# Finishing the blocks of one half inside the next half's loop (layers 1 and 2 of a four-layer graph network)

## The chip, the cores and the metric

The kernel runs on one core of a Trainium2 chip. The engines of the core work side by side, each from its own queue: PE (TensorE) multiplies matrices into banks of the accumulation memory, DVE (VectorE) and ACT (ScalarE) do elementwise work, POOL (GpSimd) does some small operations and issues some transfers, SP (SyncE) issues the transfers of the big rows. Sixteen DMA engines carry all transfers. The metric is the device time of one execution in microseconds (us): 891.3 us as the median of three runs (887.4 to 891.43) before the change. The profiled execution took 884.95 us, with a span of 883.1 us in its trace.

## The reference

There are 2708 nodes with 128 features each, and a dense 0/1 matrix `adj` of 2708 x 2708 in float32. Four layers follow each other, each of the form x = x + layer(relu(layernorm(x))). The change touches layers 1 and 2:

```
# layer 1
adj_hat = adj + eye
d = (rowsum(adj_hat) + 1e-8) ** -0.5
out = relu(((d[:,None] * adj_hat * d[None,:]) @ h) @ weight)      # x += out

# layer 2
deg = rowsum(adj), 0 replaced by 1
agg = adj.T @ h / deg[:,None]
g = agg @ W_n.T + b_n + h @ W_c.T + b_c
out = relu(gamma * (g - mean(g)) / sqrt(var(g) + 1e-5) + beta)    # mean, var over nodes; x += out
```

Layer 0 is an attention layer, whose row sums of `adj` give the degrees. Layer 3 is another attention layer, in which sorting by a score takes the place of a dense product of exponentials; it takes more than half of the time, and the change leaves it alone.

## The kernel before, in words

The 2708 rows of the matrix are cut into T = 22 row tiles of 128 (the last has 20), and the 2708 columns into six blocks of 512 (the last has 148). One block is one accumulation bank.

A product of layers 1 and 2 runs in `product_by_halves`. The columns are taken in two halves: half 0 is blocks 0 to 2 (1536 columns), half 1 is blocks 3 to 5 (1172 columns). In each half a loop goes over the 22 row tiles. For each tile the rows of `adj` (or of its transpose) are loaded (768 KB or 586 KB), converted to a rounded float type [...], and multiplied into the three banks of the half. The node features h stand as the stationary operand, cut into a high and a low part (`h_hi`, `h_lo`, written by `cut_in_two`), so each block takes two matmuls per tile (line 225).

The loads land in eight buffers in turn: three in `dflat`, one in `row_b` (layer 1) or `hn` (layer 2), and four of the pool `raws`. The transfers are issued by SP in program order (line 77). The conversion on line 525 takes turns between ACT and DVE (the first five of a layer are all on ACT) and writes to the pool `ring` of six buffers; a load buffer is free as soon as it is converted. The conversions keep their program order. Everything else is placed on the engines' queues by a scheduler that may move it.

The first 18 tiles of a half are multiplied tile by tile; the last four (NLAST) are loaded together and multiplied block by block. After its last four tiles each block is finished:

- In layer 1 `finish1` evacuates the bank to `yT` (lines 216 and 218, DVE for odd and ACT for even blocks), multiplies by the weight (line 571, PE), scales and applies relu (line 573, ACT), adds to x (line 575, DVE), and does the layer norm of the next layer. That is: statistics on DVE (lines 185 and 186), variance plus epsilon (173, DVE), the power -0.5 (174, POOL), the shift (190, DVE), and scaled relu on ACT (192). The result `h2` (in `hs`) is the features of layer 2, which `cut_in_two` (lines 501 and 502, DVE) then splits.
- In layer 2 `finish2` multiplies the bank by 1/degree of each column (line 602, DVE, from `row_a`), multiplies by the two weights (604 and 605, PE), adds the bias (606, ACT), and takes statistics (607, DVE). It needs `hT`, the transposed features, which `turn` makes from `h2` by PE transposes (199) and a copy (598).

At the start of layer 1 `finish0` does the last step of layer 0 block by block: transposes, division by the denominators (557), and the layer norm, with a factor `dis` multiplied in on DVE (189). Block 0 is done before the loop, the others at every fourth tile.

`row_a`, which only `finish2` needs, holds 1/degree along the columns, the same in every partition. It is made by two transfers that POOL issues at the head of the layer: line 484 writes `rdeg` (128 partitions x 22 numbers, node t*128+p at [p, t]) to the memory outside in the order of the nodes, 2816 pieces of 4 bytes; line 485 reads it back into all partitions (1354 KB). The second waits for the first to land.

Of the kernel before, what the change touches and what calls it, by code (L numbers as in the profile page):

```python
# [8 lines left out]
F32 = mybir.dt.float32  # L9
# [10 lines left out]
def kernel(  # L20
# [19 lines left out]
    nc = tc.nc  # L40
    P = 128
    N, D = x.shape
    assert D == P
    T = -(-N // P)
# [11 lines left out]
    TILES = [range(c // P, min(c // P + 4, T)) for c, _ in E0]  # L56
# [3 lines left out]
    NLAST = 4  # L60
# [19 lines left out]
    def cols(t):  # L80
        return slice(t * P, (t + 1) * P)
# [7 lines left out]
    small = ctx.enter_context(tc.tile_pool(name="small", bufs=2))  # L89
# [4 lines left out]
    def bank():  # L94
        return ps.tile([P, 512], F32, tag="bank", name="bank")
# [14 lines left out]
    ident = const.tile([P, P], F32, name="ident")  # L110
# [7 lines left out]
    def load(name, shape, src, queue):  # L118
        t = const.tile(shape, F32, name=name)
        queue.dma_start(t, src)  # L120
        return t
# [36 lines left out]
    hn = big.tile([P, T, D], F32, name="hn")  # L158
# [3 lines left out]
    row_a = big.tile([P, NPAD], F32, name="row_a")  # L162
# [18 lines left out]
    def layernorm(b, dst, factor=None):  # L181

        ts = slice(TILES[b][0], TILES[b][-1] + 1)
        for t in TILES[b]:
            nc.vector.bn_stats(st[:, t, :], xs[:, t, :])
            nc.vector.bn_aggr(mv[:, t, :], st[:, t, :])
        inv_sqrt(rstd[:, ts], mv[:, ts, 1], 1e-5)
        if factor is not None:
            nc.vector.tensor_mul(rstd[:, ts], rstd[:, ts], factor[:, ts])
        nc.vector.scalar_tensor_tensor(shift[:, ts], mv[:, ts, 0], -1.0, rstd[:, ts], ALU.mult, ALU.mult)  # L190
        for t in TILES[b]:
            nc.scalar.activation(
                dst[:, t, :], xs[:, t, :], AF.Relu, bias=shift[:, t : t + 1], scale=rstd[:, t : t + 1]
            )
# [25 lines left out]
    def aggregate(stationary, moving, accs, start, stop, blocks=range(NB), at=0):  # L220
        parts = stationary if isinstance(stationary, list) else [stationary]
        for b in blocks:
            lo, hi = E0[b]
            for i, w in enumerate(parts):
                nc.tensor.matmul(  # L225
                    accs[b][:, : hi - lo],
                    w,
                    moving[:, lo - at : hi - at],
                    start=start and i == 0,
                    stop=stop and i == len(parts) - 1,  # L230
                )
# [14 lines left out]
                aggregate(stationary(t), a, accs, False, t == order[-1], [b])  # L246
            finish(b, accs[b])

    def product_by_halves(order, stationary, load, finish, extra, after):

        for h, (h0, _) in enumerate(COLS):
            blocks = range(3 * h, 3 * h + 3)
            accs = {b: acc_bank(b) for b in blocks}
            for i, t in enumerate(order[:-NLAST]):
                a = load(t, h)
                aggregate(stationary(t), a, accs, i == 0, False, blocks, h0)
                if t // 4 in blocks:
                    extra(t, accs)
                after(i, h)
            last = [(t, load(t, h)) for t in order[-NLAST:]]  # L260
            for b in blocks:
                for t, a in last:
                    if t in TILES[b]:
                        extra(t, accs)
                    aggregate(stationary(t), a, accs, False, t == order[-1], [b], h0)
                finish(b, accs[b])

    with ExitStack() as stack:
        stream = stack.enter_context(tc.tile_pool(name="stream", bufs=NSTREAM))
# [22 lines left out]
        for b in range(NB):  # L292
            layernorm(b, hn)
            p = bank()
            turned(p, hn, TILES[b])
            nc.vector.tensor_copy(hT[:, spans(b)], p[:, : len(TILES[b]) * P])
            p = acc_bank(b % 2)
# [29 lines left out]
        accs = [acc_bank(b) for b in range(NB)]  # L327
# [13 lines left out]
        for t in range(T):  # L341
            a = first_rows[t] if t < 3 else load_rows(adj, t)
# [48 lines left out]
        p = bank()  # L391
# [20 lines left out]
        rdeg = const.tile([P, T], F32, name="rdeg")  # L412
# [17 lines left out]
    rdeg_d = dram.tile([NPAD], F32, name="rdeg_d")  # L430
# [49 lines left out]
    def rest(exact, stack3):  # L480

        nc.gpsimd.dma_start(rdeg_d.rearrange("(t p) -> p t", p=P), rdeg)
        nc.gpsimd.dma_start(row_a[:, :N], rdeg_d[:N].partition_broadcast(P))
        s12 = stack3.enter_context(ExitStack())
        ring = s12.enter_context(tc.tile_pool(name="ring", bufs=6))
        raws = s12.enter_context(tc.tile_pool(name="raws", bufs=4))
        h2 = hs[:, :, :P]
# [7 lines left out]
        def cut_in_two(h, b):  # L497

            if exact:
                ts = slice(TILES[b][0], TILES[b][-1] + 1)  # L500
                nc.vector.tensor_copy(h_hi[:, ts, :], h[:, ts, :])
                nc.vector.tensor_sub(h_lo[:, ts, :], h[:, ts, :], h_hi[:, ts, :])  # L502

        def halves_of(h):
            return lambda t: [h_hi[:, t, :], h_lo[:, t, :]] if exact else [h[:, t, :]]
# [26 lines left out]
        next_row = loader(adj_t, [*three, row_b[:, :CUT]], 3)  # L532
# [32 lines left out]
        def finish1(b, acc):  # L565
            evacuate(b, yT, acc)
            n = len(TILES[b])
            p = bank()
            o = stage.tile([P, 4, P], F32, tag="o", name="o", bufs=2)
            for q, t in enumerate(TILES[b]):  # L570
                nc.tensor.matmul(p[:, cols(q)], yT[:, cols(t)], w1_sb, start=True, stop=True)
            for q, t in enumerate(TILES[b]):
                nc.scalar.activation(o[:, q, :], p[:, cols(q)], AF.Relu, scale=dis[:, t : t + 1])
            ts = slice(TILES[b][0], TILES[b][-1] + 1)
            nc.vector.tensor_add(xs[:, ts, :], xs[:, ts, :], o[:, :n, :])
            layernorm(b, h2)

            for o in {3: (3,), 5: (4, 5)}.get(b, ()):
                cut_in_two(h2, o)

        def after1(i, h):

            if h == 1 and i in (5, 9, 13):
                cut_in_two(h2, i // 4 - 1)

        product_by_halves(range(T), halves_of(hn), load_plus_one, finish1, plus_one, after1)


        bias = small.tile([P, 1], F32, tag="bias", name="bias")
# [1 line left out]
        st2 = small.tile([P, NB, 6], F32, tag="st2", name="st2", bufs=1)  # L591
        tot = small.tile([P, 8], F32, tag="tot", name="tot", bufs=1)
        def turn(i, h):
            if i in (2, 4, 6):
                b = 3 * h + i // 2 - 1
                p = bank()
                turned(p, h2, TILES[b])
                nc.vector.tensor_copy(hT[:, spans(b)], p[:, : len(TILES[b]) * P])
# [8 lines left out]
            nc.vector.bn_stats(st2[:, b, :], row_b[:, lo:hi])  # L607

        next_row = loader(adj, [*three, hn.rearrange("p t d -> p (t d)")[:, :CUT]])
        product_by_halves(range(T), halves_of(h2), next_row, finish2, lambda t, accs: None, turn)  # L610
        nc.vector.bn_aggr(tot[:, 0:2], st2)
        inv_sqrt(tot[:, 4:5], tot[:, 1:2], 1e-5)
        nc.vector.tensor_mul(tot[:, 5:6], vecs[:, 2:3], tot[:, 4:5])
# [42 lines left out]
        with tc.tile_pool(name="tab", bufs=1) as tab, tc.tile_pool(name="tabs", bufs=2) as tabs:  # L656
# [17 lines left out]
            for b in range(NB):  # L674
# [4 lines left out]
                p = acc_bank(b % 2)  # L679
# [10 lines left out]
                p = acc_bank(2 + b % 2)  # L690
# [10 lines left out]
                for c in range(new.start, new.stop, 3):  # L701
# [8 lines left out]
                    p = acc_bank(4)  # L710
# [5 lines left out]
            for c in range(0, T, 3):  # L716
# [9 lines left out]
                for q in range(m):  # L726
                    t = c + q
# [15 lines left out]
                    o = (t % 4) * P  # L743
# [5 lines left out]
            p = bank()  # L749
# [33 lines left out]
            accs = [acc_bank(b) for b in range(3)]  # L783
# [72 lines left out]
            p = acc_bank(3)  # L856
# [4 lines left out]
            p = acc_bank(4)  # L861
# [10 lines left out]
            p = acc_bank(3)  # L872
# [32 lines left out]
            def sums_before(name, x):  # L905
# [45 lines left out]
            order = row("order")  # L951
# [20 lines left out]
                tag="w3",  # L972
# [21 lines left out]
            p = acc_bank(4)  # L994
# [121 lines left out]
        accs = [acc_bank(b) for b in range(NB)]  # L1116
# [89 lines left out]
        for b in range(NB):  # L1206
            evacuate(b, y_t, accs[b])
            p = bank()
# [91 lines left out]
```

## Time and profile before

| stretch of the trace (us) | what runs | length |
|---|---|---|
| 0 to 204 | layer 0 | 204 |
| 204 to 227.4 | start of layer 1, up to the first tile's matmul | 23.4 |
| 227.4 to 264.4 | layer 1, half 0 | 37.0 |
| 264.4 to 278.5 | its blocks are finished | 14.1 |
| 278.5 to 311.3 | layer 1, half 1 | 32.8 |
| 311.3 to 324.1 | its blocks are finished | 12.8 |
| 324.1 to 358.6 | layer 2, half 0 | 34.5 |
| 358.6 to 391.4 | its blocks, and layer 2, half 1 | 32.8 |
| 391.4 to 883.1 | end of layer 2, layer 3 | 491.7 |

The page gives, for the whole span, the busy share of each engine: PE 84%, DVE 66%, ACT 61%, POOL 22%. These are means over stages that differ, so the stages have to be read one by one. In a timeline, a line gives the start in us, the length, the engine, the line of the kernel, the operation, output<-input with sizes, and how many instructions are merged; in brackets stands how long the engine idled before, and what ended that idle time. In the windows a line gives, for a stretch A:B, its length and the busy time of each engine with the number of instructions, then the granted clock of PE as a share of full speed, the busy share of the DMA engines, and the GB/s that they moved.

### The profile page before, as it was taken

How to read it: one execution, taken by the hardware profiler on the slowest of the kernel's cores; microseconds unless marked ns; L12 is line 12 of the kernel's file. 1: busy time of each engine (PE TensorE's matmuls, PEld its weight loads, DVE VectorE, ACT ScalarE, POOL GpSimd, SP SyncE). 2: the span in 40 equal slices, each digit the busy share in tenths (PEclk: the TensorE clock that was granted, in tenths of full speed). 3: DMA queues.
4: the chain of work that ended last, by engine and by line, in shares of the span. 5: the costliest groups of instructions: out<-in, count | busy, mean ns of one | idle time of the engine just before them, and what ended most of it. 6: DMA issues, size and time to landing. Idle time of an engine off the chain costs nothing.

```text
span 883.1 us, 8728 instructions
## 1 busy us (share of the span) xinstructions
PE 739.1 (84%) x2980; PEld 428.5 (49%) x2980; DVE 580.9 (66%) x1097; ACT 536.9 (61%) x595; POOL 196.0 (22%) x161
## 2 busy tenths in 40 slices
PE   3599999992695979987759986389999999989996
PEld 2333333341584857665324321255555555545785
DVE  5599888893734442437986987457666666664844
ACT  3899999991846363437780024278878877866100
POOL 3000000011201010002000011456766665630010
PEclk9799999995796979997679998689999999999999
DMA  8053455707996959996501985477777777785994
GB/s 328 2 190 135 180 189 189 296 11 117 336 394 235 366 207 407 374 381 248 192 0 64 389 326 195 171 290 279 280 269 268 266 267 265 273 319 221 417 427 141
DMA packets 39506, 218.61 MB, mean 248 GB/s; under 512 B 5150, under 2 KB 14030, under 8 KB 25390
## 3 DMA queue, kind: packets, MB, share of 16 engines
q1 hardware_dynamic: 27704, 150.19, 45.4%
q0 software_dynamic: 8656, 65.76, 20.4%
q10 hardware_dynamic: 3090, 1.99, 0.7%
q8 instruction: 26, 0.43, 0.2%
q14 instruction: 30, 0.25, 0.1%
HBM read 214.12 MB, written 3.79 MB: 247 GB/s over the span
## 4 chain that ended last, share of the span: by engine, by line
PE 14%; DMA 11%; DVE 9%; POOL 7%; issue 7%; ACT 5%; POOLq 0%; DVEq 0%; ACTq 0%
DMA hs<-in_adj_t_dram 4%; PE acc L797 3%; PE bank L1178 3%; PE acc L1122 2%; DMA row_b<-pre_d,pre_i 2%; DMA yT<-pre_d,pre_i 2%; POOL hs L634 2%; ACT rows L1140 2%; PE acc L225 2%; POOL hT L634 2%; PE bank L1068 1%; DVE bits L731 1%; POOL yT L634 1%; POOL row_b L634 1%; POOL xw L634 1%
## 5 line engine op out<-in xcount | busy, mean ns | idle before, releaser
L1178 PE MATMUL bank<-rows,d_hi 128*128 128x512 f32 (+1 forms) x264 | 107.4, 411 | 38.4 <-DVE d_hi L1147 17.7
L225 PE MATMUL acc<-rows,h_hi 128*128 128x512 f32 (+1 forms) x264 | 102.7, 395 | 17.2 <-ACT rows L525 16.1
L1122 PE MATMUL acc<-e,xw 128*128 128x512 f32 (+1 forms) x264 | 104.3, 545 | 0.0
L1183 ACT ACTIVATE ln<-bank,tiny 128x512 f32<-128x512 f32 x132 | 79.5, 632 | 32.4 <-PE bank L1178 32.2
L1178 PE MATMUL bank<-rows,d_lo 128*128 128x512 f32 (+1 forms) x264 | 99.0, 386 | 0.0
L225 PE MATMUL acc<-rows,h_lo 128*128 128x512 f32 (+1 forms) x264 | 97.8, 385 | 0.2 <-DVE h_lo L502 0.2
L1178 PEld LDWEIGHTS bank<-rows,d_hi 128*128 128x128 f32 x264 | 51.6, 195 | 67.8 <-ACT ln L1183 31.3
L1186 DVE TENSOR_TENSOR e<-e,ln 128x1536 f32<-128x1536 f32 (+2 forms) x66 | 69.7, 1095 | 19.3 <-ACT ln L1183 19.1
L352 DVE SCALAR_TENSOR_TENSOR tau<-tau,e_hi,a 128x1536 f32<-128x1536 f32 (+1 forms) x44 | 70.6, 1623 | 9.7 <-DMA a<-in_adj_dram 5.9
L1122 PEld LDWEIGHTS acc<-e,xw 128*128 128x128 f32 x264 | 48.5, 191 | 52.5 <-issue 52.5
L349 ACT ACTIVATE tau<-row_a,e_neg,e_lo 128x1536 f32<-128x1536 f32 (+1 forms) x44 | 65.7, 1504 | 3.0 <-PE bank L361 2.8
L225 PEld LDWEIGHTS acc<-rows,h_hi 128*128 128x128 f32 x264 | 52.1, 197 | 30.1 <-ACT rows L525 19.3
L361 PE MATMUL bank<-tau,ones_at 128*32 128x512 f32 (+1 forms) x264 | 51.8, 566 | 8.3 <-DVE tau L352 8.3
L225 PEld LDWEIGHTS acc<-rows,h_lo 128*128 128x128 f32 x264 | 52.0, 197 | 10.1 <-DVE h_lo L502 0.7
L225 PE MATMUL acc<-yT,hs 128*128 128x512 f32 x132 | 55.8, 560 | 0.0
L1192 ACT ACTIVATE e<-e 128x2708 f32<-128x2708 f32 x22 | 54.2, 2463 | 2.2 <-DVE e L1186 2.2
L225 PE MATMUL acc<-row_b,hs 128*128 128x512 f32 x132 | 55.3, 557 | 0.0
L1178 PEld LDWEIGHTS bank<-rows,d_lo 128*128 128x128 f32 x264 | 51.9, 197 | 7.0
L225 PE MATMUL acc<-rows,y_hi 128*128 128x512 f32 x132 | 49.2, 380 | 5.0 <-DVE rows L1255 3.1
L525 ACT CAST rows<-dflat 128x1536 fp32r<-128x1536 f32 (+1 forms) x26 | 34.2, 1332 | 24.9 <-DMA dflat<-in_adj_dram 13.9
L225 PE MATMUL acc<-rows,y_lo 128*128 128x512 f32 x132 | 47.7, 377 | 0.0
L1161 DVE TENSOR_SCALAR xw<-xw,c_exp 128x128 f32<-128x128 f32 x22 | 6.6, 298 | 57.8 <-DMA xw<-xw_d,xw_i 57.8
(406 smaller groups left out, 1418.4 us busy)
## 6 DMA issues: line engine op xcount, KB each, us to landing
a<-in_adj_dram SPq DMA_DIRECT2D x21, 1354.0 KB
rows<-in_adj_t_dram SPq DMA_DIRECT2D x17, 1354.0 KB
dflat<-in_adj_t_dram SPq DMA_DIRECT2D x9, 768.0 KB
rows<-in_adj_t_dram SPq DMA_DIRECT2D x9, 768.0 KB
dflat<-in_adj_dram SPq DMA_DIRECT2D x9, 768.0 KB
rows<-in_adj_dram SPq DMA_DIRECT2D x9, 768.0 KB
dflat<-in_adj_t_dram SPq DMA_DIRECT2D x5, 1354.0 KB
hs<-in_adj_t_dram SPq DMA_DIRECT2D x5, 1354.0 KB
```

Of the source, the lines that this page charges most:

```text
L225: nc.tensor.matmul(accs[b][:, : hi - lo], w, moving[:, lo - at : hi - at], start=start and i == 0, stop=stop and i == len(parts) - 1,)
L349: nc.scalar.activation(tau[:, :w], row_a[:, h0:h1], AF.Relu, bias=e_neg[:, t : t + 1], scale=e_lo[:, t : t + 1])
L352: nc.vector.scalar_tensor_tensor(tau[:, :w], tau[:, :w], e_hi[:, t : t + 1], a[:, h0:h1], ALU.add, ALU.mult)
L361: nc.tensor.matmul(den[g : g + 32, : hi - lo], ones_at[:, b // GR, :], tau[:, lo - h0 : hi - h0], start=(t == 0 and b < GR), stop=(t == T ...
L525: m = nc.vector.tensor_copy(r, a) if i % 2 and i > 4 else nc.scalar.copy(r, a)
L634: return nc.gpsimd.indirect_dma_start(out=out, out_offset=None, in_=src, in_offset=bass.IndirectOffsetOnAxis(ap=idx, axis=0),)
L797: nc.tensor.matmul(accs[b][64 * h : 64 * h + 2 * NC, : hi - lo], wts[:r, t, :], a[:r, lo:hi], start=(t == 0), stop=(t == T - 1),)
L1122: m = nc.tensor.matmul(accs[b][:, : hi - lo], xw, e[:, lo:hi], start=(s == 0), stop=(s == NE - 1))
L1178: m = nc.tensor.matmul(num[:, : hi - lo], d, a[:, lo:hi], start=(i == 0), stop=(i == len(products) - 1))
L1183: nc.scalar.activation(ln[:, lo:hi], num[:, : hi - lo], AF.Ln, bias=tiny)
L1186: tc.keep_in_program_order(nc.vector.tensor_sub(e[:, beg:hi], e[:, beg:hi], ln[:, beg:hi]))
L1192: tc.keep_in_program_order(nc.scalar.activation(e, e, AF.Exp))
```

## The change

Two things are changed.

First, the blocks of a half are no longer finished at its end. The half ends with all 22 tiles in order, and the finishing of its three blocks is put in a list `ends`. The next half's loop, of the same layer or of the next one, takes one entry of the list after its tiles 1, 4 and 7. Only the very last half (half 1 of layer 2) still takes its last four tiles block by block and finishes its own blocks. The purpose is that the loads and products of the next half go on while a block is finished. As blocks 3 to 5 of layer 1 are then finished in layer 2's first half, `turn` is moved from tiles 2, 4, 6 to tiles 10, 12, 14, and `cut_in_two` for them goes into `finish1`.

Second, 1/degree leaves in another form. PE transposes `rdeg` to 22 partitions x 128 numbers, DVE copies it out of the bank, and POOL writes it as 22 rows of 512 bytes. In the program this stands after tile 2 of layer 1's first half, and the broadcast into `row_a` after tile 16 of its second half.

```diff
-    def product_by_halves(order, stationary, load, finish, extra, after):
+    def product_by_halves(stationary, load, finish, extra, after, ends, last):
         for h, (h0, _) in enumerate(COLS):
             blocks = range(3 * h, 3 * h + 3)
             accs = {b: acc_bank(b) for b in blocks}
-            for i, t in enumerate(order[:-NLAST]):
+            at_end = NLAST if last and h else 0
+            for t in range(T - at_end):
                 a = load(t, h)
-                aggregate(stationary(t), a, accs, i == 0, False, blocks, h0)
-                if t // 4 in blocks:
+                aggregate(stationary(t), a, accs, t == 0, t == T - 1, blocks, h0)
+                if t // 4 in blocks and t < T - 1:
                     extra(t, accs)
-                after(i, h)
-            last = [(t, load(t, h)) for t in order[-NLAST:]]
-            for b in blocks:
-                for t, a in last:
-                    if t in TILES[b]:
-                        extra(t, accs)
-                    aggregate(stationary(t), a, accs, False, t == order[-1], [b], h0)
-                finish(b, accs[b])
+                if t == T - 2 and (T - 1) // 4 in blocks:
+                    extra(T - 1, accs)
+                if ends and t in (1, 4, 7):
+                    ends.pop(0)()
+                after(t, h)
+            if at_end:
+                rest = [(t, load(t, h)) for t in range(T - at_end, T)]
+                for b in blocks:
+                    for t, a in rest:
+                        aggregate(stationary(t), a, accs, False, t == T - 1, [b], h0)
+                    finish(b, accs[b])
+            else:
+                ends += [lambda b=b, acc=accs[b]: finish(b, acc) for b in blocks]
...
-        nc.gpsimd.dma_start(rdeg_d.rearrange("(t p) -> p t", p=P), rdeg)
-        nc.gpsimd.dma_start(row_a[:, :N], rdeg_d[:N].partition_broadcast(P))
...
             layernorm(b, h2)
-            for o in {3: (3,), 5: (4, 5)}.get(b, ()):
-                cut_in_two(h2, o)
-        def after1(i, h):
-            if h == 1 and i in (5, 9, 13):
-                cut_in_two(h2, i // 4 - 1)
-        product_by_halves(range(T), halves_of(hn), load_plus_one, finish1, plus_one, after1)
+            if b >= 3:
+                cut_in_two(h2, b)
+        def after1(t, h):
+            if (t, h) == (2, 0):
+                p = bank()
+                nc.tensor.transpose(p[:T, :P], rdeg, ident)
+                by_tile = small.tile([T, P], F32, tag="by_tile", name="by_tile", bufs=1)
+                nc.vector.tensor_copy(by_tile, p[:T, :P])
+                nc.gpsimd.dma_start(rdeg_d.rearrange("(t p) -> t p", p=P), by_tile)
+            if (t, h) == (16, 1):
+                nc.gpsimd.dma_start(row_a[:, :N], rdeg_d[:N].partition_broadcast(P))
+            if h == 1 and t in (6, 10, 14):
+                cut_in_two(h2, t // 4 - 1)
+        ends = []
+        product_by_halves(halves_of(hn), load_plus_one, finish1, plus_one, after1, ends, False)
...
         def turn(i, h):
-            if i in (2, 4, 6):
-                b = 3 * h + i // 2 - 1
+            if i in (10, 12, 14):
+                b = 3 * h + i // 2 - 5
...
-        product_by_halves(range(T), halves_of(h2), next_row, finish2, lambda t, accs: None, turn)
+        product_by_halves(halves_of(h2), next_row, finish2, lambda t, accs: None, turn, ends, True)
```

## The prediction

> **What bounds the kernel now.** I first read the slices of the span: around slices 10, 13 and 15 PE and DMA both sink. The windows by stage then give the shares. The six stretches are layer 1's first half, the gap after it, its second half, the gap before layer 2, and layer 2's two halves (columns: length, busy time of PE, weight loads, DVE, ACT, POOL, clock, DMA share, GB/s):
>
> ```profile
> 227.40:264.40 37.00, 35.66 (x159) 29.26 (x159) 19.78 (x60) 24.50 (x31) 4.17 (x4) 0.93 0.97 365
> 264.40:278.50 14.10, 3.15 (x26) 2.77 (x25) 8.49 (x37) 9.98 (x27) 3.02 (x3) 0.69 0.45 169
> 278.50:311.30 32.80, 32.25 (x168) 27.33 (x168) 11.76 (x25) 13.15 (x15) 2.04 (x2) 0.92 0.98 368
> 311.30:324.10 12.80, 6.72 (x20) 3.50 (x20) 8.50 (x30) 7.20 (x18) 1.75 (x3) 0.75 0.36 150
> 324.10:358.60 34.50, 32.63 (x133) 25.94 (x134) 8.87 (x11) 17.09 (x12) 1.38 (x1) 0.95 0.97 372
> 358.60:391.40 32.80, 32.28 (x154) 24.59 (x154) 13.29 (x20) 14.54 (x14) 1.08 (x1) 1.00 0.94 365
> ```
>
> Inside a half PE is full and DMA nearly so. The gaps are chains: PE idles 10.6 us in the first, some 6 us in the second. Ahead of all this lies a dead stretch, in the timeline of 203 to 226 us:
>
> ```profile
> 204.67 1.61 POOL L484 DMA_DIRECT2D rdeg_d<-rdeg  x1 [3.46 <-issue]
> ...
> 207.35 0.16 DVE L173 TENSOR_SCALAR isq<-mv 128x4 f32<-128x4 f32 x1
> ...
> 221.12 0.60 POOL L485 DMA_DIRECT2D row_a<-rdeg_d  x1 [14.84 <-DMA rdeg_d<-rdeg]
> 221.75 2.02 POOL L174 TENSOR_TENSOR rstd<-isq,neg_half 128x4 f32<-128x4 f32 x2
> 222.81 0.16 DVE L189 TENSOR_TENSOR rstd<-rstd,dis 128x4 f32<-128x4 f32 x1 [12.90 <-POOL rstd L174]
> ```
>
> The power for block 0's normalisation (L174) has its input at 207.5 us, but stands on POOL's queue behind the issue of the broadcast (L485), which waits until the 4-byte scatter (L484) has landed. DVE, ACT and PE all wait for that power. The first gap is a chain too:
>
> ```profile
> 264.38 1.98 PE L571 MATMUL bank<-w_sb,yT 128*128 128x128 f32 x16
> 266.76 1.16 PE L571 MATMUL bank<-w_sb,yT 128*128 128x128 f32 x8 [0.40 <-ACT o L573]
> 278.47 0.79 PE L225 MATMUL acc<-rows,h_hi 128*128 128x512 f32 x1 [10.55 <-ACT rows L525]
> ```
>
> The tile PE waits for is a mere conversion (L525) of rows that landed long ago; it stands on ACT behind three blocks' normalisations.
>
> **What the Trainium skill says.** "DMA: Bandwidth & Descriptors", section Specifications: below 512 B a transfer runs under line rate. The trace agrees: the 11 KB of L484 took 15.9 us in 4-byte pieces. The same page, section Latency and other measured facts: about 2 us fixed cost per DMA; here the 64 KB gathers land in 2.6 us at the median. "TensorE: Matmul & The Clock Gate", section "Architectural detail: the array is 16× 32×32, not 1× 128×128": the queues of ACT and DVE are strictly first in, first out, GpSimd's too for each of its processors; both waits above agree. Its section What's actually happening: an idle window of about 3.4 us halves the clock, a busy one restores it. Here the clock was 0.50 by 272 us, 4 us into the gap, and the first tile after it ran at half rate.
>
> **The change, part by part.**
>
> *1. 1/degree.* Removed: the 4-byte scatter. Added: one transpose (4 such took 1.1 us), one copy of 22x128 (under 0.2 us), a transfer of 22 rows. I looked at the order in which the changed kernel's instructions are built: the scheduler does not leave the broadcast at tile 16 but puts it early again. POOL's queue reads: power block 0, rows out, power block 1, broadcast, power block 2. So block 0 no longer waits for any transfer, and the broadcast still falls in the ramp. The rows' landing is not in the trace: bounds are 2.6 us (the gather) and 15.9 us (the old scatter). I take 2.6, since 22 pieces replace 2,816. Then block 2's power is held until about 214.5, and block 2 serves only tile 8, which PE reaches at 213 + 8 x 1.6 = 226.
>
> Start of PE: from the power's start (221.75) to the first tile (227.39) passed 5.64 us. Now the power starts at 207.4, so PE starts at 213.0, 14.4 us earlier. The eight tiles in flight were asked for by 207.8; eight less the three already there are 3.9 MB, 9.4 us at the 418 GB/s of the full windows, so they are in at about 214. I take off 0.6 us, because DVE used the old wait to prepare part of block 1 and 2: 13.8 us. The half itself stays PE's: 22 tiles x 1.36 us, plus 12 x 0.2 for the identity, plus transposes of five blocks at 1.1 is near the 37.0 measured.
>
> *2. End of layer 1's first half* (X = its last matmul, 264.4 before). The text says "a block at tiles 1, 4, 7", but the built order is different. PE: block 0's weight product, tiles 0 and 1, the products of blocks 1 and 2, then tile 2. ACT: outputs and normalisation of block 0, conversions of tiles 2 and 4, outputs of blocks 1 and 2, normalisation of block 1, tile 6, normalisation of block 2, tile 8. So conversions still queue behind normalisations. Walked with the trace's durations (evacuation 0.58, product 1.16, outputs 1.14, add 0.68, statistics 1.3, power 1.0, normalise 1.65, conversion 1.17 on ACT and 0.77 on DVE, tile 1.15):
>  - PE: product to X+1.2, tiles 0 and 1 to X+3.5, products to X+5.9.
>  - Block 0: outputs to X+2.8, add and statistics to 4.8, power 6.1, normalised 8.1, tile 2 converted 9.2. PE idles 3.4 us.
>  - Outputs of block 1 follow at X+11.4; DVE's add, a cut of h2 into high and low that waits for PE's tile 3, statistics and power bring tile 5 to about X+17.4 and, with tiles 2 and 3 at half clock (+1.5), X+18.9. PE idles another 4 us. Block 2 likewise holds tile 8 to X+25.
>  - Then PE is free: tile 11 ends at X+30, and ten tiles at 1.36 end the half at X+43.5.
>
> Before, the same point is at 311.2, X+46.8, with the products of blocks 3 and 4 (2.3 us) already inside. Gain 3.3 us, of which 2.3 return below.
>
> *3. Layer 1 to 2* (Y = that end). PE: tile 0, products of blocks 3 to 5 around tile 1, the twelve transposes of `turn` hoisted to here, then tile 2. ACT gives tile 2's conversion (1.48 us in this half) only after block 3's normalisation: outputs to Y+7.6, power 10.2, normalised 12.2, converted 13.7, the tile at half clock from Y+14.7. Twenty tiles x 1.36, two `wc` products of 1.05 and about 1.4 more for half clock and a wait for tile 5 end the half at about Y+45.3. Before it took 358.6 - 311.2 = 47.4, with less of these products in it. Both halves together: 94.2 us before, 43.5 + 45.3 = 88.8 now: 5.4 us.
>
> *4. Layer 2's end.* `finish2` of blocks 0 to 2 moves among the tiles: 4 products of 1.05 that stood in front of the half, now inside. PE was full there (32.28 of 32.80), so they cost the same in either place. Rows come at 1.4 us a tile against PE's 1.15 plus these, and lead by several tiles: nought. The last four tiles are as before.
>
> Sum: 13.8 + 5.4 = 19.2 us. 891.3 - 19.2 = 872.1. Layer 3 hangs on layer 2's last block and shifts whole.
>
> **The rivals.**
>  - *The ends overlap fully.* PE's idle 10.6 and 6 us, and some 4 us of half clock, vanish too: 14 + 20.6, 857 us. For it: 97% DMA shows loads would follow, and rings are deep. Against it: the built order above, with ACT and DVE first in, first out.
>  - *Only the start gains.* The scattered waits of PE at each boundary equal the old gap, or the clock halves once more in each (2 us): 14 less 0 to 4, 877 to 881 us. For it: the chain of one block is some 8 us and three now run one after another, where the old order ran three nearly together.
>  - *Slower.* The rows land no faster than the old scatter: issued at 211.5, landed at 227.4, tile 8 then at 232 instead of 226, loss 6; and each boundary costs 9 us more than before, because three block chains in series stand before tile 8: 891.3 - 13.8 + 6 + 18 = 901 us. Against it: piece count, and blocks 0 and 1 pass ahead of that wait.
>
> **How the numbers follow.** Forecast (about 866 to 876 us) 0.55, full overlap 0.17, start alone 0.22, slower or no change 0.06. The range 857 to 881 reaches to the middle of the second and the end of the third, and leaves out some 0.17. The landing of the rows (2.6 to 15.9) costs nothing at one end and 6 us at the other, inside it. Faster by over 0.5% (below 886.8) takes all of the first three and a little is kept back: 0.93; same 0.03; slower 0.04.
>
> **What would show it.** In the trace after: no POOL wait above 4 us before the first power, PE's first tile near 213 us; the old 10.55 us idle on a conversion split into two or three of 2 to 5 us, each put down to ACT or DVE `rows`, DVE `shift` waiting for POOL behind them; layer 2's first half ending near 339, its last matmul near 372. It is wrong if PE runs through the boundaries without such waits (then about 857), if tile 8 of the first half waits for POOL, or if single waits grow past 6 us.

## The result, and the profile after

The changed kernel took 863.5 us (median of 4 runs, 861.0 to 865.7), against 890.6 for the kernel before on the same chip: ratio 0.970 (0.966 to 0.974). Run again beside the experiments it took 863.95 against 884.56, ratio 0.976 (0.971 to 0.981). Measured in pairs the gain is thus 27 and 21 us; it is the kernel before whose median moved (884.6 to 890.6 over the chips used here), not the changed one. The traces say where the gain is made (ends of the tile loops, in us from the span's start):

| end of | before | after | gain so far | forecast |
|---|---|---|---|---|
| wait for the first tile (its matmul starts) | 227.4 | 212.6 | 14.8 | 14.4 |
| layer 1, half 0 | 264.5 | 253.6 | 10.9 | 13.8 |
| layer 1, half 1 | 311.2 | 294.8 | 16.4 | 17.1 |
| layer 2, half 0 | 358.6 | 338.5 | 20.1 | 19.2 |
| layer 2, half 1 | 391.4 | 370.6 | 20.8 | 19.2 |
| span | 883.1 | 860.4 | 22.7 | 19.2 |

What follows layer 2's loop is the same code in both and took 491.7 and 489.8 us; over all thirteen traces of this study it took 487.4 to 494.8. So a whole time says less about this change than the stretch up to 391 us does, and below I read both. One run is left out below: of the four of the kernel called *GpSimd free*, one took 891.4 us at a granted clock of 0.82, where the others show 0.94.

The windows of the kernel after, one for each half with the boundary ahead of it inside (same columns as in the prediction):

```profile
212.60:253.60 41.00, 37.75 (x164) 29.87 (x165) 22.58 (x75) 25.10 (x32) 6.12 (x7) 0.92 1.00 389
253.60:294.80 41.20, 34.03 (x177) 29.01 (x177) 17.98 (x52) 22.02 (x38) 4.11 (x4) 0.92 0.85 304
294.80:338.50 43.70, 38.83 (x170) 30.47 (x169) 19.13 (x51) 25.32 (x34) 4.40 (x4) 0.92 0.98 380
338.50:370.60 32.10, 31.81 (x154) 24.69 (x154) 13.68 (x20) 13.25 (x13) 1.08 (x1) 1.00 0.94 376
```

Two things are to be seen. In the first line DMA is at 1.00 and PE no longer full (37.75 of 41.00; before it was 35.66 of 37.00): this half now runs at what its transfers give. In the second DMA falls to 0.85 and PE to 34 of 41: the boundary still costs something there.

The start of layer 1 after, in the timeline:

```profile
207.99 1.01 POOL L174 TENSOR_TENSOR rstd<-isq,neg_half 128x4 f32<-128x4 f32 x1 [6.46 <-DVE isq L173]
...
210.99 0.86 POOL L591 DMA_DIRECT2D rdeg_d<-by_tile  x1 [2.00 <-DVE mv L186]
...
212.62 1.22 PE L225 MATMUL acc<-rows,h_hi 128*128 128x512 f32 x2 [0.77 <-ACT rows L529]
```

The first block's power starts at 208.0 instead of 221.75, ahead of any transfer of GpSimd's, and PE starts at 212.6. The boundary between the halves of layer 1, PE's waits in its timeline:

```profile
262.24 0.50 PE L225 MATMUL acc<-rows,h_hi 128*128 128x512 f32 x1 [3.45 <-ACT rows L529]
270.52 0.80 PE L225 MATMUL acc<-rows,h_hi 128*128 128x512 f32 x1 [3.02 <-DVE rows L529]
276.29 0.51 PE L225 MATMUL acc<-rows,h_hi 128*128 128x512 f32 x1 [0.69 <-ACT rows L529]
```

In place of one wait of 10.55 us there are three, 7.2 us together. ACT's timeline beside it shows why:

```profile
254.76 1.16 ACT L577 ACTIVATE o<-bank,dis 128x128 f32<-128x128 f32 x4
259.49 1.65 ACT L192 ACTIVATE hs<-xs,shift,rstd 128x128 f32<-128x128 f32 x4 [3.57 <-DVE shift L190]
261.04 2.22 ACT L529 CAST rows<-dflat 128x1172 fp32r<-128x1172 f32 x2
263.17 2.15 ACT L577 ACTIVATE o<-bank,dis 128x128 f32<-128x128 f32 x8
269.82 1.65 ACT L192 ACTIVATE hs<-xs,shift,rstd 128x128 f32<-128x128 f32 x4 [4.50 <-DVE shift L190]
```

ACT stands idle for 3.57 and 4.50 us ahead of a normalisation (L192) whose shift is not there yet, and the conversion PE wants (L529, at 261.0) is queued behind it. In this time the buffers are not given back: from 263.6 to 270.5 us the load queue issues nothing, and DMA moves 0 to 19 GB/s from 268.5 to 271.

### The profile page after: what moved, and what is told of

The parts are those of the page before. It is cut to its first block, busy times and chain, and to the rows that moved or that the text cites. A ratio compares the mean times of both kernels' runs of the same rounds, so it can differ in the third digit from the quotient of the medians.

```text
span 860.4 us, 8730 instructions
## 1 busy us (share of the span) xinstructions
PE 737.2 (86%) x2981; PEld 427.3 (50%) x2981; DVE 580.9 (68%) x1098; ACT 536.0 (62%) x595; POOL 191.8 (22%) x161
## 4 chain that ended last, share of the span: by engine, by line
PE 17%; DMA 11%; DVE 10%; issue 6%; POOL 5%; ACT 5%; POOLq 0%; DVEq 0%; ACTq 0%
PE bank L1191 5%; DMA hs<-in_adj_t_dram 4%; PE acc L1135 4%; DMA row_b<-pre_d,pre_i 4%; PE acc L810 3%; ACT rows L1153 2%; PE acc L225 2%; PE bank L1081 2%; POOL hs L647 1%; POOL hT L647 1%; DVE bits L744 1%; POOL xw L647 1%; POOL row_b L647 1%; ACT e L1205 1%; DMA hs<-in_adj_t_dram,row_i 1%
## 5 line engine op out<-in xcount | busy, mean ns | idle before, releaser
L1191 PE MATMUL bank<-rows,d_hi 128*128 128x512 f32 (+1 forms) x264 | 105.6, 404 | 37.9 <-DVE d_hi L1160 17.4
L225 PE MATMUL acc<-rows,h_hi 128*128 128x512 f32 (+1 forms) x264 | 105.8, 405 | 11.6 <-ACT rows L529 6.3
L1199 DVE TENSOR_TENSOR e<-e,ln 128x1536 f32<-128x1536 f32 (+2 forms) x66 | 69.7, 1096 | 14.8 <-ACT ln L1196 14.4
L529 ACT CAST rows<-dflat 128x1536 fp32r<-128x1536 f32 (+1 forms) x26 | 34.2, 1330 | 20.2 <-DMA dflat<-in_adj_t_dram 9.7
```

The costliest lines, as they stand in the source:

```text
L225: nc.tensor.matmul(accs[b][:, : hi - lo], w, moving[:, lo - at : hi - at], start=start and i == 0, stop=stop and i == len(parts) - 1,)
L529: m = nc.vector.tensor_copy(r, a) if i % 2 and i > 4 else nc.scalar.copy(r, a)
L1191: m = nc.tensor.matmul(num[:, : hi - lo], d, a[:, lo:hi], start=(i == 0), stop=(i == len(products) - 1))
L1199: tc.keep_in_program_order(nc.vector.tensor_sub(e[:, beg:hi], e[:, beg:hi], ln[:, beg:hi]))
```

## The experiments

Theory, formed after the result: the gain is in two parts that add up. The 22 rows give some 11 to 15 us at the start, and the interleaved ends some 8 to 10, of which the rest is still lost to conversions that stand behind normalisations. Rivals: that the start is worth only what PE gains in starting earlier (the queue wait), against the small pieces themselves being in the way; and that the rows come too late at the boundaries, whatever the order. "Less" below is by the ratio to the kernel before on the same chip. The last five columns are stage ends in the trace.

| kernel | us | ratio (95%) | first tile | L1 h0 | L1 h1 | L2 h0 | L2 h1 |
|---|---|---|---|---|---|---|---|
| before | 884.6 to 890.6 | 1 | 227.4 | 264.5 | 311.2 | 358.6 | 391.4 |
| after, again | 863.95 | 0.976 (0.971 to 0.981) | 213.9 | 254.8 | 296.4 | 340.1 | 372.3 |
| rows only | 871.6 | 0.983 (0.979 to 0.986) | 212.8 | 253.5 | 300.8 | 347.3 | 380.1 |
| ends only | 883.6 | 0.995 (0.991 to 0.998) | 231.0 | 268.2 | 311.1 | 354.9 | 387.0 |
| late broadcast | 883.8 | 0.996 (0.994 to 0.997) | 214.1 | 265.9 | 312.4 | 359.6 | 392.4 |
| rows at the head | 871.6 | 0.985 (0.978 to 0.991) | 218.3 | 254.4 | 301.6 | 348.3 | 381.2 |
| staged | 865.2 | 0.974 (0.971 to 0.977) | 212.4 | 251.5 | 295.0 | 340.6 | 372.7 |
| lead alone | 855.0 | 0.964 (0.960 to 0.969) | 213.0 | 252.8 | 290.1 | 330.1 | 362.2 |
| as written | 906.9 | 1.023 (1.019 to 1.028) | 213.6 | 254.1 | 314.1 | 383.9 | 418.7 |
| evacuation first | 856.6 | 0.968 (0.964 to 0.972) | 212.9 | 252.0 | 288.3 | 332.3 | 364.4 |
| GpSimd free | 856.7 | 0.964 (0.958 to 0.969) | 214.1 | 254.3 | 287.9 | 330.4 | 362.5 |
| staged, all free | 859.5 | 0.969 (0.966 to 0.972) | 213.5 | 254.5 | 292.1 | 333.6 | 365.7 |

### One half of the change at a time

*Rows only*: the kernel before, with the new form and place of 1/degree (the change's lines at tiles 2 and 16 of layer 1), and the blocks finished as before.

> The kernel before, with 1/degree leaving as 22 rows and nothing else changed. Theory A (the gain is the wait on POOL's queue at the head plus some at the ends of the halves): the first tile of layer 1 starts near 213 us instead of 227.4, the layer's first half ends 11 to 14 us earlier, all later stages keep their lengths, so 11 to 14 us less (about 877 to 880 us, ratio 0.984 to 0.988). Theory B (the start gave little, the overlapped ends gave nearly all): under 6 us less. Theory C (part of the gain lies in layer 3): more than 16 us less, with layer 3 shorter than 489 us in the trace.

*Ends only*: the changed kernel, with the 4-byte scatter and the broadcast back at the head.

```diff
+        nc.gpsimd.dma_start(rdeg_d.rearrange("(t p) -> p t", p=P), rdeg)
+        nc.gpsimd.dma_start(row_a[:, :N], rdeg_d[:N].partition_broadcast(P))
...
-            if (t, h) == (2, 0):
...
-            if (t, h) == (16, 1):
```

> The changed kernel, with the old 4-byte transfer and the broadcast back at the head. Theory A: the start stays as it was, from the end of layer 1's first half to layer 2's last matmul 117 us instead of 127, so 8 to 11 us less than before (ratio 0.988 to 0.991). My forecast's own sum for this part was 5.4 us. Theory B: 20 us or more. Theory D (overlap is worth nothing by itself, and needs the early start): within 3 us of before.

Rows only took 15.4 us off, ends only 4.8: the first lies a little above the 11 to 14 of its theory A, the second below the 8 to 11. In the traces, layer 2 ends 11.3 us earlier with the rows alone, and what follows it is not shorter than 489 us (489.8), so that theory C finds no support. With the ends alone the stretch from layer 1's first half's end to layer 2's end is 118.8 us against 126.9 before, 8.1 less, but that run had lost 3.7 us by the end of the first half: its scatter kept GpSimd waiting for 18.27 us, where it was 14.84 before. Whether that loss is chance, one trace of each cannot tell. Without it the parts add up, 11.3 + 8.1 = 19.4 against the 20.8 of the whole change; the times, which contain it, give 15.4 + 4.8 = 20.2 against the 21 and 27 of the whole.

### What of 1/degree cost the time

*Late broadcast*: the kernel before, whose scatter stays at the head in 4-byte pieces, while the broadcast that waits for it goes behind all powers of the first half. The wait on GpSimd's queue is gone, the pieces are kept.

```diff
         nc.gpsimd.dma_start(rdeg_d.rearrange("(t p) -> p t", p=P), rdeg)
-        nc.gpsimd.dma_start(row_a[:, :N], rdeg_d[:N].partition_broadcast(P))
...
+            if (i, h) == (16, 0):
+                tc.keep_in_program_order(nc.gpsimd.dma_start(row_a[:, :N], rdeg_d[:N].partition_broadcast(P)))
```

> The kernel before, with the 4-byte transfer still at the head, but the broadcast that waits for it issued behind the last power of layer 1's start. It tells what the 4-byte transfer costs by itself. If the cost was only the wait in POOL's queue: the first tile starts near 213 to 215 us, as with rows, and the time equals that of the rows-only kernel within 3 us. If the 2,816 small pieces hold up the loads of the rows too: the first half is stretched by up to 8 us, so 4 to 8 us above the rows-only kernel. If the pieces were all: no gain over before.

*Rows at the head*: the other corner. The pieces are gone, and a wait is kept, though a shorter one: transpose, copy, 22 rows and broadcast stand where scatter and broadcast stood, and GpSimd waits 5.14 us ahead of the broadcast, where it was 14.84 before.

```diff
-        nc.gpsimd.dma_start(rdeg_d.rearrange("(t p) -> p t", p=P), rdeg)
+        p_deg = bank()
+        nc.tensor.transpose(p_deg[:T, :P], rdeg, ident)
+        by_tile = small.tile([T, P], F32, tag="by_tile", name="by_tile", bufs=1)
+        nc.vector.tensor_copy(by_tile, p_deg[:T, :P])
+        nc.gpsimd.dma_start(rdeg_d.rearrange("(t p) -> t p", p=P), by_tile)
         nc.gpsimd.dma_start(row_a[:, :N], rdeg_d[:N].partition_broadcast(P))
```

> The kernel before with only the form of 1/degree changed and its place kept: transpose, copy, 22 rows and broadcast all stand at the head, so the broadcast still waits for the rows ahead of the first block's power. It is the fourth corner beside the late broadcast (pieces kept, wait gone: about 4 us less than before) and the rows in their new place (pieces gone, wait gone: 15.4 less). GpSimd's idle before the broadcast also bounds how long the rows take to land. Theory one (the 2,816 pieces keep the loads off the DMA engines, and this is nearly the whole cost): the first half ends at 253 to 257 us and the time is 12 to 16 us less than before. Rival (what counts is when PE can start): PE starts at 217 to 220 us, 5 us later than with the rows in their new place, and 8 to 11 us are gained.

The stretch of 208 to 224 us in the windows, first of the late broadcast, then of the rows at the head:

```profile
208.00:224.00 16.00, 11.10 (x42) 8.81 (x42) 11.97 (x68) 8.77 (x12) 5.23 (x5) 0.64 0.97 78
```

```profile
208.00:224.00 16.00, 8.56 (x29) 6.51 (x28) 11.77 (x67) 9.13 (x13) 5.20 (x5) 0.52 1.00 381
```

Both show DMA engines busy throughout (0.97 and 1.00), but one moved 78 GB/s and the other 381. A part of the 381 is the broadcast, which comes later with the late broadcast. The queue of the big loads alone moved 1.24 MB and 4.67 MB in these 16 us (queue, kind: packets, MB, share of the 16 engines; in the same order):

```profile
q1 hardware_dynamic: 232, 1.24, 91.7%
```

```profile
q1 hardware_dynamic: 855, 4.67, 77.9%
```

With the late broadcast PE starts at 214.1, 13.3 us earlier than before, runs through the tiles that have landed, starves, and ends the half at 265.9: later than before. With the rows at the head PE starts only at 218.3, 5.5 us after rows only, and ends the half at 254.4, 0.9 after it. From its start on it is full:

```profile
218.30:254.40 36.10, 35.56 (x160) 29.46 (x159) 18.96 (x57) 24.14 (x30) 4.74 (x4) 0.93 1.00 384
```

So two limits lie on this half: its rows have to land, and PE has some 35.6 us of work from its start on. Before, both came out near 264 to 266 us. Taking away the wait alone leaves the rows late (late broadcast). Taking away the pieces alone, with the whole wait kept, would leave PE's work: from 227.4 us on it would end near 263 us. That is an estimate, 227.4 + 35.6, since no run keeps the whole wait without the pieces. The 22 rows take both limits away, and this is worth 11 us; between a start at 213 and one at 218 only 0.9 us differ.

Against what was expected: the late broadcast is 12.2 us above rows only, more than the 4 to 8 expected if the pieces hold up the loads; the rows at the head took 13.6 us less than before, as their theory one has it. The late broadcast also took 4.0 us less than before in time, which its trace does not show (layer 2 ends at 392.4 against 391.4). The traced run of the kernel before, 884.95 us, was shorter than its median on that chip, 887.9, so one trace of each does not settle a difference of this size.

"DMA: Bandwidth & Descriptors" of the Trainium skill, section "Queues, rings and completion order", says that a DMA engine takes turns between its queues a packet at a time; that would let pieces stand between the packets of the loads. The GB/s above agree with it, but no run here shows the turns themselves. The issues of the rows at the head also give the landing that the prediction had to bound (KB, median us):

```profile
rdeg_d<-by_tile POOLq DMA_DIRECT2D x1, 11.0 KB, 5.3
```

The same 11 KB took 15.9 us in 4-byte pieces.

### What is left at the boundaries

*Lead alone*: the changed kernel, whose conversions are written four tiles ahead of their products. A block is still finished in one piece.

```diff
-                a = load(t, h)
+                k = (2 * last + h) * T + t
+                while taken[0] <= min(k + min(LEAD, max(0, k - 16)), 4 * T - 1):
+                    ahead.append(load(taken[0]))
+                    taken[0] += 1
+                a = ahead.pop(0)
```

> After, with one edit: a tile's conversion is written four tiles ahead of its products, so that the conversions stand further forward on the queues of ACT and DVE; the finishing of a block is still one piece. Theory one (what was left at the two boundaries is conversions queued behind normalisations): the 15.4 us of PE's waits for rows there halve, 855 to 859 us. Rival (the rows themselves come too late, since the transfers are near 418 GB/s): no gain, 861 to 865 us.

It took 855.0 us, 8.9 less than the changed kernel beside it on the same chip. PE's waits at the two boundaries, from 252 us to the end of layer 2's first half (us in total, times, longest), first of the changed kernel, then of lead alone:

```profile
PE acc L225 <- ACT rows L529: 4.4, 3, 3.5
PE bank L199 <- DVE hT L611: 3.9, 1, 3.9
PE acc L225 <- DVE rows L529: 3.0, 1, 3.0
```

```profile
PE acc L225 <- DVE rows L535: 3.9, 6, 1.4
PE acc L225 <- ACT rows L535: 3.1, 4, 1.4
PE bank L199 <- DVE hT L624: 0.4, 1, 0.4
```

and layer 1's second half and layer 2's two halves in its windows:

```profile
252.80:290.10 37.30, 32.09 (x177) 26.89 (x175) 19.11 (x52) 21.87 (x38) 4.61 (x4) 1.00 0.96 353
290.10:330.10 40.00, 37.47 (x169) 28.74 (x170) 19.43 (x51) 25.23 (x34) 4.09 (x4) 1.00 1.02 406
330.10:362.20 32.10, 31.82 (x154) 24.68 (x154) 13.72 (x20) 13.36 (x13) 1.08 (x1) 1.00 0.96 388
```

The waits for rows hardly shrank in sum (7.4 us, then 7.0): four became ten short ones, and the wait for `hT` went. None is over 1.5 us, so the clock stays at 1.00 where it was 0.92, the buffers keep coming back, and DMA goes from 304 to 353 and from 380 to 406 GB/s. The expected time was right, and the expected mechanism (half of the waits gone) only in part. The 15.4 us of waits named there are those of the whole stretch of 204 to 380 us (6.3 and 5.2 for rows, 3.9 for `hT`); at the boundaries they were 11.3 with the one for `hT`, and 7.4 are left. Of the 7.6 us by which these two halves became shorter than in the first trace of the changed kernel, 3.5 are the wait for `hT`, and 3.3 are PE's busy time (34.03 + 38.83, then 32.09 + 37.47), since the clock no longer falls.

*As written*: the changed kernel, with every engine bound to the program's order, so that a block is finished at the tile where the text says so.

> After, with every engine bound to the order in which the program is written in layer 1's second half and layer 2's first: a block's evacuation, product, outputs, statistics and normalisation then really stand behind tile 1, 4 or 7, and not three blocks together. Theory one: tiles 2, 5 and 8 each wait for a whole chain of 8 to 9 us, of which two tiles cover little: some 5 us more per block, 875 to 885 us. Rival (it is the bunching by the scheduler that costs): 852 to 858 us.

It took 906.9 us, more than the 875 to 885 expected. PE's waits of 204 to 400 us:

```profile
PE acc L243 <- ACT rows L550: 31.2, 6, 8.3
PE acc L243 <- DVE rows L550: 20.9, 5, 9.0
```

52 us in eleven waits. Six of them, 5.7 to 9.0 us long and 45 us in sum, stand at the six blocks: every block's chain lies open before the tiles behind it. The scheduler's order, whose bunching the prediction held against the change, takes 43 us less than the order of the text; how much of this is the bunching and how much the other instructions it moves, no run tells apart.

*Staged*: conversions four tiles ahead, a block finished in four steps one tile apart, four tiles from block to block, all engines bound to that order.

```diff
-            layernorm(b, h2)
...
+            return [product1, added, normed, cut]
...
+                        ends.setdefault(4 * j + i if not last else 1 + 3 * j, []).append(f)
```

> The changed kernel, with each block's finishing cut into four steps (product; outputs and statistics; normalisation; cut) that follow one another at one tile's distance, four tiles between blocks, with conversions four tiles ahead of PE, and with the order of the program kept on every engine in layer 1's second and layer 2's first half. If what is left at the boundaries is conversions queued behind normalisations (theory A): the waits of 3.5, 3.0 and 3.9 us and the half clock after them go, 10 to 15 us less than the changed kernel (848 to 854 us). If DMA is the limit there [...]: under 4 us less. If the kept order costs more than it brings: slower.

It missed: 865.2, no better than the changed kernel. The waits of 240 to 380 us show none on rows over 0.3 us, and a new one (with 2.7 us more on DVE's evacuations):

```profile
PE bank L613 <- ACT yT L243: 12.9, 3, 5.8
```

The evacuation of a bank (L243) now stood on ACT behind conversions whose rows had not landed, and PE, bound to its order, stood behind the product that needs it. *Evacuation first* mends this: all banks are evacuated at the half's end ahead of those conversions, and a block takes six steps (product, outputs, statistics, shift, normalisation, cut), blocks five tiles apart.

```diff
+                    if not last:
+                        evacuate(b, yT, accs[b])
...
-            return [product1, added, normed, cut]
+            return [product1, outputs, added, shifted, normed, cut]
```

> The staged form mended: there all of PE's waits were for evacuations that stood on ACT and DVE behind conversions whose rows had not landed (12.9 and 2.7 us). Here all three banks are evacuated at the half's end ahead of those conversions, and a block is finished in six steps one tile apart (product, outputs, add and statistics, shift, normalise, cut), blocks five tiles apart. Theory one (the order on ACT and DVE is all that is left): PE has no wait over 1 us at the boundaries, the 15.5 us of waits and some 4 us of half clock go: 844 to 852 us. Rival (rows are then the bound: 49 MB from 253 us on at 418 GB/s, less what was loaded ahead): 852 to 858 us. If neither, about 863 as after.

856.6 us, in the rival's range, though not for its reason alone. (The rows of the three halves from 253 us on are 42 MB, 2708 rows of 1172, 1536 and 1172 columns of 4 bytes, not the 49 written there.) Its first boundary is nearly free (PE busy for 23.16 of the 24.00 us up to 276), but then the loads stop. GpSimd in its timeline, the load queue in its waits:

```profile
277.56 1.01 POOL L193 TENSOR_TENSOR rstd<-isq,neg_half 128x4 f32<-128x4 f32 x1 [6.77 <-DVE isq L192]
278.52 0.64 POOL L649 DMA_DIRECT2D row_a<-rdeg_d  x1
279.15 1.09 POOL L94 MEMSET row_b<- 128x1172 f32 x1
```

```profile
SPq L96 <- POOL row_b L94: 12.2, 1, 12.2
```

The last tile has 20 rows, so GpSimd zeroes its buffer ahead of the load. Bound to the program's order, this zeroing stood behind the third block's power and the broadcast, and all later loads stood behind it on SP's queue, for 12.2 us. *GpSimd free* binds only PE, DVE and ACT; *staged, all free* binds none.

> The mended staged form with one edit: GpSimd's queue is no longer bound to the program's order, only those of PE, DVE and ACT. There the zeroing of the last tile's buffer stood on GpSimd behind the third block's power and the broadcast, and the load queue stood 12.2 us behind that zeroing, while DMA fell to 105 GB/s over 276 to 282 us. Theory one (this wait is what kept the mended form from its 844 to 852): the hole closes and some 4 to 7 us go, 848 to 853 us. Rival (layer 2's first half is the transfers' anyway, 16.6 MB at 418 GB/s is 39.8 us): 855 to 858 us.

> The mended staged form with no engine bound to an order: the scheduler places the six steps as it likes. Theory one (the steps as written are also a good order for the scheduler, and the zeroing goes early): 848 to 853 us, as with GpSimd alone set free. Rival (the scheduler bunches the blocks again, as it does in the changed kernel): 855 to 863 us.

The hole shrinks: in the windows, evacuation first and then GpSimd free.

```profile
276.00:282.00 6.00, 4.19 (x23) 3.52 (x23) 4.57 (x12) 2.71 (x5) 2.68 (x3) 0.92 0.35 105
```

```profile
276.00:282.00 6.00, 5.96 (x37) 5.14 (x35) 4.27 (x14) 3.17 (x7) 1.01 (x1) 1.00 0.76 262
```

Layer 2 ends 2 us earlier (362.5 against 364.4). The medians are the same (856.7 and 856.6), but were taken on two chips; the ratios, 0.964 and 0.968, have intervals that overlap. So the wait on the zeroing cost 2 us in the traces. The time lies in the range of the rival for that run, but cannot tell no gain from one of a few us. With nothing bound it is 859.5. Lead alone, evacuation first and GpSimd free end layer 2 within 2.2 us of each other, and their intervals overlap; the simplest of them, lead alone, is the version to keep. After it PE is busy for 101.4 of the 109.4 us from 252.8 to 362.2, and the 42 MB of rows alone take 100 us at 418 GB/s (an estimate). In layer 2's first half the transfers are the limit (DMA at 1.02), in its second half PE is (31.82 of 32.10), so more order would bring 8 us at most.

## Why the prediction was right, and where it was not

- *Sum and direction.* 872 us with 857 to 881 were forecast, 863.5 measured. In the trace up to layer 2's end the forecast was 19.2 us and the gain 20.8. That these are so near is luck in part: the start gave 2.9 us less than forecast, the boundaries 3.8 more, the last half 0.7 more. The rest of the way from 872 to 863.5 is the kernel before, whose median was 891 for the forecast and whose traced run took 885, and layer 3's own spread of 7 us.
- *Part 1, the start: PE's start was right, the half behind it was not.* The first power, PE's start (212.6, forecast 213.0) and the broadcast's place came as described. The step that failed is "the half itself stays PE's": it took 41.0 us, not 37.0, with DMA at 1.00, so of 14.8 us at the start 10.9 were left at the half's end (13.8 forecast). PE was busy 2.1 us longer and idle 1.9 us longer in it. The sum that was not made is that of the rows: the half has 16.6 MB, which at the 418 GB/s that the prediction used take 39.8 us. Before, 37.0 us were enough, although DMA was at 0.97, because eight of the 22 tiles had been asked for before the pause and landed in it; that head start went with the pause. The ten traces in which the small pieces are gone end this half at 251.5 to 254.8 us, whether PE starts at 212 or at 218.
- *The cause of the dead stretch: half of it was named.* The prediction took off the scatter and priced the wait on GpSimd's queue alone. The late broadcast took that wait away, and its trace ended the half 1.4 us later than before; the rows at the head kept a wait of 5.14 us and lost 0.9. The pieces held the loads up at the same time, and the change gained because it removed both, which the prediction did not say. What was there to be read is the GB/s beside the DMA share: in the dead stretch, from 212 to 220 us, the engines were 0.86 to 0.97 busy at 63 to 97 GB/s.
- *The rows' landing.* 2.6 was taken between 2.6 and 15.9; it was 5.3 where it was measured, and the broadcast after went out 5.7 us behind the rows' issue. PE never waited for GpSimd there. It waited once, 1.61 us at 226.4, for a conversion that stood on DVE behind shifts and cuts whose powers had been held, so at most that is the price.
- *Parts 2 and 3, the boundaries: right mechanism, sized too dear.* The first took 41.2 us against 43.5 forecast (3.45 and 3.02 us of waits, forecast 3.4 and 4; the third block held tile 8 for 0.69 only). Layer 2's first half took 43.7 against 45.3. There the wait came at another place: 3.89 us of PE on `hT`, where the transposes of `turn` wait for a bank to be copied out by DVE, and not on tile 2's conversion. The copy stood on DVE behind the blocks' statistics, so it is the same kind of queue with another piece of work in it. Together 9.2 us gained against 5.4. That the place of the conversions on these queues is what was left is shown by lead alone: moved ahead, they give 8.9 us more, though by shorter waits and a full clock, and not by fewer waits for rows.
- *Part 4.* Nought forecast, 0.7 us gained (32.8 to 32.1).
- *Full overlap, 857 us,* was the next rival, and three kernels of the study reach that time (855.0, 856.6, 856.7), though with 28 to 32 us gained and not the 34.6 of its sum, since the kernel beside them took 885 to 887 and not 891. The built order of the change did not give it. *The start alone* would be the time of rows only, 871.6 against the 877 to 881 written; by the end of layer 2 rows only gained 11.3 us, inside the 10 to 14 of that rival, and most of the rest is again the 891, where the kernel beside it took 887.9. It failed for the change because the boundaries gained too. *Slower* needed rows that land late and chains that lie open; the second is what "as written" shows, at 906.9.

What stays open: why layer 3, with the same code, takes 487 to 495 us from trace to trace; what makes GpSimd wait 14.84 us for the 4-byte scatter in one run and 18.27 in another; and where the half would end with the whole wait and no pieces, for which there is only the estimate above.

## What to carry to other kernels

When an engine waits for a tiny transfer, look at the GB/s beside the DMA share before pricing the wait: thousands of small pieces can hold up the big loads at the same time. Then each hides the other: moving the wait alone gains little (4 us here), while giving the data whole rows removes both (15). Where a block's finishing is put between tiles, what counts is where the conversions that the next tiles need stand on the same queues: write them some tiles ahead first, and only then cut up the finishing. An order bound by hand binds small things too (an evacuation, a zeroing); each of them can stop a whole queue.

## What the runs showed of the hardware that was not expected

- Beside 11 KB in 2,816 pieces of 4 bytes the big loads moved 1.24 MB in 16 us (late broadcast), and 4.67 MB beside the 22 rows and the broadcast (rows at the head), with the engines' busy share at 0.97 and 1.00: the busy share alone does not tell useful from useless work.
- As 22 rows of 512 bytes the same 11 KB landed in 5.3 us, beside running loads.
- From 290 to 330 us of lead alone DMA moved 406 GB/s at a share of 1.02, and PE, at full clock, was busy for 37.5 of the 40.0 us: there the rows come a little slower than PE uses them. "DMA: Bandwidth & Descriptors", section Specifications, puts the limit of the memory outside at about 358 GB/s for a core, as half of what two cores share. This kernel runs on one core and is above that for 40 us on end; no run here has a second core at work.
- Waits of 1.1 to 1.5 us leave the clock at 1.00, as in lead alone; waits of 3.0 to 3.9 us, as in the kernel after, were followed by 0.50. "TensorE: Matmul & The Clock Gate", section What's actually happening, has about 3.4 us for this, which agrees roughly with both. In the windows, PE's first tile behind a wait of 3.02 us in the kernel after, then behind one of 1.42 us in lead alone (the third number from the end is the clock):

```profile
270.50:271.00 0.50, 0.48 (x1) 0.48 (x2) 0.50 (x5) 0.50 (x3) 0.00 (x0) 0.50 0.00 0
```

```profile
259.50:260.00 0.50, 0.50 (x3) 0.41 (x3) 0.00 (x0) 0.50 (x3) 0.00 (x0) 1.00 0.98 403
```
